# Experts' output rows: one scatter for each piece, or summed in SBUF and scattered block by block

## The chip, the core and the metric

The kernel runs on one core of a Trainium2 chip, in one launch. The metric is device time in microseconds (us); smaller is better. PE is the matrix engine (TensorE), PEld its loading of the stationary operand, DVE VectorE, ACT ScalarE, POOL GpSimd, SP SyncE, which here only issues DMAs.

## What is computed

Two transformer layers on 1024 rows (32 x 32) of 256 float32 values. Each layer is an attention block and a feed-forward block:

```python
x = x + _L0_attn_ref(_L0_cond_ref(x, ...), ...)
x = x + _L0_ffn_ref(_L0_cond2_ref(x, ...), ...)
x = x + _L1_attn_ref(_L1_cond_ref(x, ...), ...)
x = x + _L1_ffn_ref(_L1_cond2_ref(x, ...), ...)
```

The change touches the last one, `_L1_ffn_ref`: a mixture of 16 experts with hidden width 128, of which each row uses two, and a shared expert that every row uses.

```python
probs = softmax(xt @ Wr.T + bias)                # 1024 x 16
topk_val, topk_idx = top_k(probs, 2)
w = topk_val / (sum(topk_val) + 1e-9)
g = einsum('th,ehi->tei', xt, Wg)                # hidden width i = 128
u = einsum('th,ehi->tei', xt, Wu)
y = einsum('tei,eih->teh', silu(g) * u, Wd)
routed = einsum('tke,tk,teh->th', one_hot(topk_idx), w, y)
shared = (silu(xt @ sWg) * (xt @ sWu)) @ sWd
return routed + shared
```

## The kernel before

**Blocks and pieces.** Only the two experts of a row are computed. The 1024 rows with two experts each make 2048 gated rows, sorted by expert and cut into NB = 16 blocks of P = 128. An expert's rows may begin and end inside a block, so one block may need several experts. A *piece* is one block with one expert. Going through blocks and experts in order, as in a merge, there are always NP = 16 + 16 - 1 = 31 pieces. Piece j is of expert `ex[j]` and of block `j - bx[j]`; both numbers come from the data, are computed on the chip into `eb` and loaded into registers of PE and DVE. A piece runs all 128 rows of its block through its expert, and only the rows that belong to this expert are used afterwards.

**Before the loop.** The attention rows that the experts work on go out to `od` in DRAM (`rows_out`, tile `o`). `tok_` has the row number of each sorted row, `slot_` tells whether the expert was the row's first or second choice. `pick(b)` lets POOL gather the 128 rows of block b from `od` into `xg[b]` (L1469): nine gathers in front of the loop, the other seven in the loop, each behind one piece's products. All experts' weights stand in SBUF as `ew` (6 MB).

**The loop over pieces** (one turn of `for j in range(NP)` each):

- For j < 16, PE turns block j of `xg` (`xt`, L1565) and DVE copies it to `xT` (L1567). These 16 turns are called the first half here, the other 15 the second.
- DVE copies the piece's block out of `xT` to `xs` (L1576), with an address from a register.
- PE multiplies it by gate and up weights into `gu` (L1579, two instructions in the code, four in the trace), the weights' address from a register.
- ACT takes the Silu (`hb`, L1591), DVE multiplies by the up half (`hb`, L1592). These are the gated rows.
- PE turns them (`ht`, L1594), ACT copies the result (`hT`, L1596).
- PE multiplies by the down weights into `y` (L1598); its PSUM pool `yp` has two buffers.
- DVE (odd pieces, L1601) or ACT (even pieces, L1603) copies `y` to `yb`, one of 12 buffers.
- POOL scatters `yb` to the rows of `ys_d` in DRAM (L1608), one row for each token and choice. The row numbers are column k of `to`; rows that belong to another piece of the block have a number beyond the table and are dropped by the bounds check.

`places()` computes `to` from the sorted order on DVE (L1519 to L1544), at piece 2.

**The shared expert** is done in two halves of 512 rows. `shared_in(n)` makes gate and up products, Silu and product (L1325 to L1341), `shared_out(n)` the four down products and their addition to `acc`, which already holds the rest of the sum (L1347, L1351). Half 0 is begun ahead of the loop, with the product of its hidden rows on POOL (L1338), and added at piece 2. Half 1 comes with the loop's end.

**The end.** `weigh()` makes the two weights of each row. Eight DMAs load `ys_d` back, 128 tokens with both choices each (L1628, in turn on the SP and the ACT queue). Sixteen DVE instructions multiply by the weights and add to `acc` (L1632), and eight DMAs write the output (L1635).

**The order of instructions** on each engine comes from a scheduler that sees all of the program. The code adds orders where it wants others: `behind(first, *later)` says that each of `later` stands behind `first` in its engine's queue, with no wait of its own, and `products` writes a sum of products in one bank. `declare_no_dep` says that two instructions with overlapping memory are not to wait for each other. Pools hand their buffers out in turn, so an instruction also waits for the last reader of its buffer.

Of the kernel before, what the change touches and what calls it, by code (L numbers as in the profile page):

```python
# [128 lines left out]
def tile_layers(ctx: ExitStack, tc: tile.TileContext, i: dict, out: bass.AP):  # L129
# [60 lines left out]
    def products(groups, ends=None):  # L190


        last = None
        for ps, pairs in groups:
            for j, (a, b) in enumerate(pairs):
                mm_ = te.matmul(ps, lhsT=a, rhs=b, start=j == 0, stop=j == len(pairs) - 1)  # L196
                if j == 0 and last is not None:
                    tc.add_manual_dep(mm_.ins, last.ins.name, in_order, reason="one open sum per bank")
            last = mm_
            if ends is not None:  # L200
                ends.append(mm_)
        return last
# [843 lines left out]
    with tc.tile_pool(name="w1", bufs=1, reuse_waits="tile") as wp:  # L1046
# [269 lines left out]
        with (  # L1316
# [3 lines left out]
            def small(name, shape, dt=F32):  # L1320
                return hp.tile(list(shape), dt, name=name)

            hs = small("h", (P, CH)), small("up", (P, CH))

            def shared_in(n, pool, tag, eng):  # L1325
                ns = slice(n * CH, (n + 1) * CH)
                pair = []
                for f in (NE, NE + P):
                    ps = pool.tile([P, CH], F32, tag=tag, name=tag)
                    products([(ps, [(wfo[:, k, f : f + P], AVT[:, k, ns]) for k in range(2)])])  # L1330
                    pair.append(ps)
# [20 lines left out]

            w12 = small("w12", (P, 2, NG))
            eb = small("eb", (1, NP), I32)
            to = small("to", (P, NP), I32)
            xT = hp.tile([P, NB, D], F32, name="xT")
            with (
                tc.tile_pool(name="mm5", bufs=3, space=bass.MemoryType.PSUM, reuse_waits="tile") as mm,
# [6 lines left out]
                def rows_out(g):  # L1365

                    po = mm.tile([P, CH], F32, tag="mm", name="mm")
                    products([(po[:, :D], [(AVT[:, k, g * P : (g + 1) * P], wo2[:, k, :]) for k in range(2)])])
                    o = sp.tile([P, D], F32, tag="o", name="o")
                    s.copy(o, po[:, :D])  # L1370
                    (nc.sync, s)[g % 2].dma_start(od[g * P : (g + 1) * P, :], o)

# [140 lines left out]
            with (  # L1513
# [3 lines left out]
                tc.tile_pool(name="y5", bufs=2, space=bass.MemoryType.PSUM, reuse_waits="tile") as yp,  # L1517
            ):
                def places():  # L1519

                    of = small("of", (P, NB, NE))
                    of_ = v.tensor_tensor(
                        of,
                        starts.unsqueeze(1).broadcast_to([P, NB, NE]),
                        C("row").unsqueeze(2).broadcast_to([P, NB, NE]),
                        ALU.is_le,
                    )
                    behind(loaded[1][-1], of_)
                    pn = small("pn", (P, NB))
                    v.tensor_reduce(pn, of, AX.X, ALU.add)  # L1530
                    v.tensor_tensor(pn, pn, C("block1"), ALU.add)
                    v.scalar_tensor_tensor(slot_, slot_, float(NT), tok_, ALU.mult, ALU.add)
                    v.tensor_scalar(slot_, slot_, -SKIP, None, ALU.add)
                    mine = small("mine", (P, NP, NB))
                    v.tensor_tensor(
                        mine,
                        pn.unsqueeze(1).broadcast_to([P, NP, NB]),
                        C("piece").rearrange("p (j b) -> p j b", b=NB),
                        ALU.is_equal,
                    )  # L1540
                    v.tensor_tensor(mine, mine, slot_.unsqueeze(1).broadcast_to([P, NP, NB]), ALU.mult)
                    tof = small("tof", (P, NP))
                    v.tensor_reduce(tof, mine, AX.X, ALU.add)
                    v.tensor_scalar(to, tof, SKIP, None, ALU.add)  # L1544

                def weigh():

# [6 lines left out]
                    v.reciprocal(su, su)  # L1554
                    v.tensor_tensor(w12, w12, su.unsqueeze(1).broadcast_to([P, 2, NG]), ALU.mult)

                put, ybs, gus = [], [], []
                for j in range(NP):
                    if j == 2:
                        places()  # L1560
                        shared_out(0, first_h, yp, "y")
                    if j < NB:
                        pt = xp.tile([P, CH], F32, tag="xt", name="xt")
                        for k in range(2):
                            turned = te.transpose(pt[:, k * P : (k + 1) * P], xg[j][:, k * P : (k + 1) * P], ident)  # L1565
                            behind(gus[j - 2] if j > 1 else loaded[0][-1], turned)
                        v.tensor_copy(xT[:, j, :], pt[:, :D])  # L1567
                    w = ew[:, bass.ds(ex[j], 1), :].rearrange("p a n -> p (a n)")
                    at_b = nc.s_assert_within(
                        j - bx[j],  # L1570
                        max(0, j - NE + 1),
                        min(j, NB - 1),
                        skip_runtime_bounds_check_because="a piece's number is its block's and its expert's together",
                    )
                    x = sp.tile([P, 1, D], F32, tag="xs", name="xs")
                    v.tensor_copy(x, xT[:, bass.ds(at_b, 1), :])  # L1576
                    pg = gp.tile([P, CH], F32, tag="gu", name="gu")
                    for k in range(2):
                        mm_ = te.matmul(  # L1579
                            pg[:, :D],  # L1580
                            lhsT=x[:, 0, k * P : (k + 1) * P],
                            rhs=w[:, k * D : (k + 1) * D],
                            start=k == 0,
                            stop=k == 1,
                        )
                    gus.append(mm_)
                    if len(xg) < NB:
                        pick(len(xg))
                        tc.add_manual_dep(picked[-1].ins, mm_.ins.name, waits, reason="no long row of gathers")
                    h = sp.tile([P, P], F32, tag="hb", name="hb")  # L1590
                    s.activation(h, pg[:, :P], AF.Silu)  # L1591
                    v.tensor_tensor(h, h, pg[:, P:D], ALU.mult)  # L1592
                    ph = tp.tile([P, CH], F32, tag="ht", name="ht")
                    te.transpose(ph[:, :P], h, ident)  # L1594
                    hT = sp.tile([P, P], F32, tag="hT", name="hT")
                    s.copy(hT, ph[:, :P])  # L1596
                    py = yp.tile([P, CH], F32, tag="y", name="y")
                    te.matmul(py[:, :D], lhsT=hT, rhs=w[:, 2 * D :], start=True, stop=True)  # L1598
                    yb = sp.tile([P, D], F32, tag="yb", name="yb", bufs=12)
                    if j % 2:  # L1600
                        v.tensor_copy(yb, py[:, :D])  # L1601
                    else:
                        s.copy(yb, py[:, :D])  # L1603
                    ybs.append(yb)
                    if j >= 2:
                        for k in range(len(put), j + 1):
                            put.append(
                                g_.indirect_dma_start(  # L1608
                                    out=ys_d,
                                    out_offset=bass.IndirectOffsetOnAxis(ap=to[:, k : k + 1], axis=0),  # L1610
                                    in_=ybs[k],
                                    in_offset=None,
                                    bounds_check=2 * NT - 1,
                                    oob_is_err=False,
                                )
                            )
                weigh()
                shared_out(1, shared_in(1, gp, "gu", v), yp, "y")
                behind(picked[-1], *put)
                for j, a in enumerate(put):  # L1620
                    for b in put[:j]:
                        tc.declare_no_dep(a.ins, b.ins, reason="a row is written by one piece")
                ys = ys_d.rearrange("(k g p) d -> g p k d", k=2, p=P)
                y2s = []
                for g in range(NG):
# [83 lines left out]
```

## Time and profile before

| what | us | from |
|---|---|---|
| median of three runs | 644.38 | 643.24, 644.38, 644.47 |
| the profiled execution, its own time | 649.91 | the run |
| span of its trace | 647.7 | the page |
| stages ahead of the last attention's end | 538 | busy time in stretches |
| routing, order of rows, first gathers | 538 to 573 | the same |
| pieces 4 to 15 | 573 to 602 | the same |
| pieces 16 to 30 | 602 to 628.5 | the same |
| last pieces' scatter, loads, weighted sums, output | 628.5 to 647.7 | the same |

Each row of the profile's groups names a line, an engine, an operation, the tiles (out<-in) with their shapes, the number of instructions, their busy time and mean length, and what ended the engine's idle time ahead of them. The rows of the last 100 us that the change touches:

```profile
L1608 POOL DMA_INDIRECT ys_d<-yb,to x31 | 30.8, 995 | 22.3 <-ACT hT L1596 7.4 <-DVE yb L1601 5.5 <-ACT yb L1603 5.0
L1576 DVE COPY xs<-xT 128x256 f32 (+1 forms) x31 | 10.3, 355 | 10.1 <-PE gu L1579 9.8 <-DVE hb L1592 0.3
L1601 DVE COPY yb<-y 128x256 f32<-128x256 f32 x15 | 6.4, 424 | 7.6 <-PE gu L1579 3.5 <-PE y L1598 3.5
L1603 ACT COPY yb<-y 128x256 f32<-128x256 f32 x16 | 6.0, 372 | 11.0 <-PE y L1598 6.6 <-remote 3.3 <-issue 1.2
L1351 DVE TENSOR_TENSOR acc<-acc,y 128x256 f32<-128x256 f32 x8 | 3.4, 421 | 1.8 <-PE y L1347 1.7
```

In a timeline a row is a time from the span's start, a length, the engine, the line, the operation and the tiles, and in brackets how long the engine was idle ahead of it and what ended that. The clock (PEclk) is the share of full speed that PE was granted.

### The profile page before, as it was taken

The page shows a single profiled execution, that of the slowest core. Times are in us where ns is not written, and L with a number is a line of the kernel's source. Part 1 is how long each engine was busy: PE and PEld are TensorE (multiplying, and loading weights), DVE is VectorE, ACT ScalarE, POOL GpSimd, SP SyncE. Part 2 cuts the span into 40 slices and gives each one's busy share as a digit, 9 for nine tenths or more (in the row PEclk, how much of TensorE's full clock was granted, in tenths as well). Part 3 has the DMA queues.
Part 4 walks back from the last instruction along what each step waited for, and adds up shares of the span by engine and source line. Part 5 has one row for each costly group of instructions (what it writes and reads, how often), then busy time and mean ns, then how long its engine had stood idle before and what let it go on. Part 6 is the DMA issues. An engine that isn't in the chain of part 4 may idle for free.

```text
span 647.7 us, 9218 instructions
## 1 busy us (share of the span) xinstructions
PE 579.4 (89%) x3302; PEld 449.0 (69%) x3302; DVE 377.9 (58%) x880; ACT 185.0 (29%) x503; POOL 195.7 (30%) x279
## 2 busy tenths in 40 slices
PE   3989999999999998999999999996788889686992
PEld 1667778688778886788878886785565666464660
DVE  4656675865956939433292139554566685642535
ACT  1312232332312213122031103233456454121440
POOL 5014001523530049950000000007465300655550
PEclk9979999999999999999999999997799989797997
DMA  6962300555441000000000046014221101221115
GB/s 176 361 214 27 64 2 26 153 128 134 116 131 39 0 14 1 1 2 17 0 1 1 1 161 293 1 54 119 57 66 58 49 2 66 74 61 46 33 50 194
DMA packets 29884, 48.47 MB, mean 75 GB/s; under 512 B 8249, under 2 KB 21966, under 8 KB 29008
## 3 DMA queue, kind: packets, MB, share of 16 engines
q1 hardware_dynamic: 19405, 30.23, 13.7%
q0 software_dynamic: 5904, 15.39, 9.2%
q10 hardware_dynamic: 4531, 2.28, 1.2%
q8 instruction: 26, 0.43, 0.3%
q14 instruction: 18, 0.15, 0.1%
HBM read 36.84 MB, written 13.01 MB: 77 GB/s over the span
## 4 chain that ended last, share of the span: by engine, by line
PE 70%; DVE 16%; issue 4%; ACT 3%; DMA 3%; POOL 2%; another core or an unknown queue 1%; ACTq 0%; SPq 0%; DVEq 0%; POOLq 0%
PE ff L196 30%; PE mm L196 11%; PE gu L1579 4%; PE y L1598 3%; PE sc L1157 3%; PE tr L477 3%; DVE vblk L427 2%; PE sc L444 2%; PE po L1191 2%; PE mm L939 2%; DVE kb L437 2%; ACT sm L1172 2%; DVE AVT L1225 1%; PE tr L470 1%; POOL xg L1469 1%
## 5 line engine op out<-in xcount | busy, mean ns | idle before, releaser
L1098 POOL DMA_INDIRECT kv<-rows_d,at x40 | 39.2, 979 | 173.8 <-DVE rsm L1012 152.3
L662 POOL COPY rr<-raw 88x256 f32<-88x256 f32 x64 | 29.4, 493 | 95.8 <-PE tr L525 48.8
L594 DVE SCALAR_TENSOR_TENSOR th<-th,ff 128x512 f32<-128x512 f32 x32 | 21.8, 683 | 38.1 <-ACT th L593 38.1
L437 DVE TENSOR_TENSOR kb<-KT,con 128x1024 f32<-128x1024 f32 x28 | 34.0, 1234 | 12.3 <-ACT KT L539 6.0
L1608 POOL DMA_INDIRECT ys_d<-yb,to x31 | 30.8, 995 | 22.3 <-ACT hT L1596 7.4
L1579 PE MATMUL gu<-ew,xs 128*128 x124 | 36.4, 415 | 0.7 <-DVE xs L1576 0.7
L593 ACT ACTIVATE th<-ff 128x512 f32<-128x512 f32 x32 | 19.1, 597 | 59.5 <-PE ff L196 56.1
L196 PE MATMUL ff<-x,w_g 128*128 128x256 f32 x128 | 35.6, 391 | 0.0
L196 PE MATMUL ff<-x,w_u 128*128 128x256 f32 x128 | 34.9, 386 | 0.0
L196 PE MATMUL ff<-y,f_w_gate 128*128 128x256 f32 x128 | 31.5, 381 | 0.0
L196 PE MATMUL ff<-y,f_w_up 128*128 128x256 f32 x128 | 31.1, 381 | 0.3 <-DVE th L594 0.3
L1172 ACT ACTIVATE sm<-sm,mx 128x160 f32<-128x160 f32 x64 | 26.8, 420 | 11.7 <-DVE mx L1170 8.6
L196 PE MATMUL ff<-h,d_Wd 128*128 128x256 f32 x128 | 29.8, 381 | 0.0
L1598 PE MATMUL y<-ew,hT 128*128 x62 | 21.9, 436 | 7.7 <-issue 4.2
L196 PE MATMUL ff<-h,f_w_down 128*128 128x256 f32 x128 | 28.3, 379 | 0.0
L1157 PE MATMUL sc<-KT,qz 128*128 128x160 f32 x128 | 25.9, 335 | 2.6 <-issue 2.4
L1579 PEld LDWEIGHTS gu<-ew,xs 128*128 128x128 f32 x124 | 24.3, 209 | 5.6 <-DVE xs L1576 1.1
L1191 PE MATMUL po<-PT,kv 128*128 128x256 f32 x64 | 19.8, 432 | 9.4 <-ACT PT L1188 7.5
L1166 DVE SCALAR_TENSOR_TENSOR sm<-bad,sc 128x320 f32<-128x320 bf16 x32 | 15.5, 485 | 21.5 <-PE sc L1157 8.0
L196 PEld LDWEIGHTS ff<-x,w_g 128*128 128x128 f32 x128 | 22.8, 189 | 7.4 <-issue 4.9
L595 DVE SCALAR_TENSOR_TENSOR h<-th,ff 128x512 f32<-128x512 f32 x32 | 21.8, 680 | 9.4 <-PE ff L196 9.1
L196 PEld LDWEIGHTS ff<-x,w_u 128*128 128x128 f32 x128 | 23.5, 190 | 5.4 <-issue 2.2
(421 smaller groups left out, 1314.5 us busy)
## 6 DMA issues: line engine op xcount, KB each, us to landing
ew<-in_L_ffn_W SPq DMA_DIRECT2D x1, 6144.0 KB
rows_d<-rr SPq DMA_DIRECT2D x32, 176.0 KB
x<-in_x SPq DMA_DIRECT2D x4, 256.0 KB
w_u<-in_L_cond_Wu SPq DMA_DIRECT2D x1, 1024.0 KB
w_g<-in_L_cond_Wg SPq DMA_DIRECT2D x1, 1024.0 KB
d_Wd<-in_L_cond_Wd SPq DMA_DIRECT2D x1, 1024.0 KB
f_w_gate<-in_L_ffn_w_gate SPq DMA_DIRECT2D x1, 1024.0 KB
f_w_up<-in_L_ffn_w_up SPq DMA_DIRECT2D x1, 1024.0 KB
```

The costliest lines, as they stand in the source:

```text
L196: mm_ = te.matmul(ps, lhsT=a, rhs=b, start=j == 0, stop=j == len(pairs) - 1)
L437: v.tensor_tensor(kb, KT[:, m, js].rearrange("p (b k) -> p b k", b=4).unsqueeze(2).broadcast_to([P, 4, 8, 32]), m8.unsqueeze(1).unsqueeze( ...
L594: v.scalar_tensor_tensor(flat(t), flat(t), 1.0, flat(pg), ALU.add, ALU.mult)
L595: v.scalar_tensor_tensor(flat(h[:, f : f + 2]), flat(t), 0.5, flat(pu), ALU.mult, ALU.mult)
L662: g_.tensor_copy(r[:, :, j].rearrange("p o g d -> p g o d"), raw[j].rearrange("p (g a o d) -> a p g o d", g=4, a=8, d=32)[a],)
L1098: got = g_.indirect_dma_start(out=kv[:, a, :], out_offset=None, in_=rows_d, in_offset=bass.IndirectOffsetOnAxis(ap=at[:, g, a : a + 1], ax ...
L1157: mm_ = te.matmul(ps[:, h, :], lhsT=q.qz[:, b, h].rearrange("p g t -> p (g t)"), rhs=q.KT[:, b, :], start=True, stop=True,)
L1172: exp_ = s.activation(sm[:, h], sm[:, h], AF.Exp, bias=mx[:, h : h + 1], accum_out=q.su[:, b, h : h + 1])
L1191: mm_ = te.matmul(q.po[:, b, : 2 * P], lhsT=q.kv[:, b, P:], rhs=PT[:, j, :], start=True, stop=False)
L1579: mm_ = te.matmul(pg[:, :D], lhsT=x[:, 0, k * P : (k + 1) * P], rhs=w[:, k * D : (k + 1) * D], start=k == 0, stop=k == 1,)
L1598: te.matmul(py[:, :D], lhsT=hT, rhs=w[:, 2 * D :], start=True, stop=True)
L1608: g_.indirect_dma_start(out=ys_d, out_offset=bass.IndirectOffsetOnAxis(ap=to[:, k : k + 1], axis=0), in_=ybs[k], in_offset=None, bounds_ch ...
```

## The change

- The pieces of one block are summed in SBUF. A new tile `yall` holds 16 blocks of 128 rows x 256 and is zeroed by four POOL memsets. For each piece a DVE instruction adds `y`, multiplied by the piece's column of `own`, to the piece's block of `yall`, whose address comes from a register. `own` has a 1 for the rows of the block that are the piece's and a 0 for the others. This instruction takes the place of the copy to `yb` on DVE or ACT.
- A block is scattered when its last piece can have been added: block b behind piece b + 15. There are 16 scatters for 31, all in the second half, with no rows left out. `to` has one column for a block. `places()` computes `own` as a maximum, loses three DVE instructions, and stands behind piece 1.
- For odd pieces j of the first half, the product `y` of piece j - 1 (`yd` at that place in the code) is ordered behind the turn `ht` of piece j's gated rows, so PE has both turns of a pair ahead of both products.
- `shared_in` takes an instruction that its products are to stand behind; for half 1 it is the last piece's `y`.
- The tile `o` takes its buffers from those of `xs`.

```diff
-            def shared_in(n, pool, tag, eng):
+            def shared_in(n, pool, tag, eng, after=None):
...
-                    products([(ps, [(wfo[:, k, f : f + P], AVT[:, k, ns]) for k in range(2)])])
+                    for k in range(2):
+                        up_ = te.matmul(ps, lhsT=wfo[:, k, f : f + P], rhs=AVT[:, k, ns], start=k == 0, stop=k == 1)
+                        if after:
+                            behind(after, up_)
...
-            to = small("to", (P, NP), I32)
+            to, own = small("to", (P, NB), I32), small("own", (P, NP))
+            yall = hp.tile([P, NB, D], F32, name="yall")
+            for b in range(0, NB, 4):
+                g_.memset(yall[:, b : b + 4, :], 0.0)
...
-                    o = sp.tile([P, D], F32, tag="o", name="o")
+                    o = sp.tile([P, 1, D], F32, tag="xs", name="o")[:, 0, :]
...
-                    v.scalar_tensor_tensor(slot_, slot_, float(NT), tok_, ALU.mult, ALU.add)
-                    v.tensor_scalar(slot_, slot_, -SKIP, None, ALU.add)
...
-                    v.tensor_tensor(mine, mine, slot_.unsqueeze(1).broadcast_to([P, NP, NB]), ALU.mult)
-                    tof = small("tof", (P, NP))
-                    v.tensor_reduce(tof, mine, AX.X, ALU.add)
-                    v.tensor_scalar(to, tof, SKIP, None, ALU.add)
+                    v.tensor_reduce(own, mine, AX.X, ALU.max)
+                    v.scalar_tensor_tensor(to, slot_, float(NT), tok_, ALU.mult, ALU.add)
...
                     if j == 2:
-                        places()
                         shared_out(0, first_h, yp, "y")
...
-                    te.transpose(ph[:, :P], h, ident)
+                    ht_ = te.transpose(ph[:, :P], h, ident)
+                    if j % 2 and j < NB:
+                        behind(ht_, yd)
...
-                    te.matmul(py[:, :D], lhsT=hT, rhs=w[:, 2 * D :], start=True, stop=True)
-                    yb = sp.tile([P, D], F32, tag="yb", name="yb", bufs=12)
-                    if j % 2:
-                        v.tensor_copy(yb, py[:, :D])
-                    else:
-                        s.copy(yb, py[:, :D])
...
+                    yd = te.matmul(py[:, :D], lhsT=hT, rhs=w[:, 2 * D :], start=True, stop=True)
+                    ys_.append((j, at_b, py))
+                    if j == 1:
+                        places()
+                    while j >= 1 and ys_:
+                        k, at_k, py = ys_.pop(0)
+                        to_k = yall[:, bass.ds(at_k, 1), :].rearrange("p a n -> p (a n)")
+                        kept_.append(
+                            v.scalar_tensor_tensor(to_k, py[:, :D], own[:, k : k + 1], to_k, ALU.mult, ALU.add)
+                        )
+                    if j >= NE - 1:
+                        b = j - NE + 1
+                        put.append(
+                            g_.indirect_dma_start(
+                                out=ys_d,
+                                out_offset=bass.IndirectOffsetOnAxis(ap=to[:, b : b + 1], axis=0),
+                                in_=yall[:, b, :],
+                                in_offset=None,
+                            )
+                        )
                 weigh()
-                shared_out(1, shared_in(1, gp, "gu", v), yp, "y")
+                shared_out(1, shared_in(1, gp, "gu", v, yd), yp, "y")
...
+                    for x in kept_[j + NE :]:
+                        tc.declare_no_dep(x.ins, a.ins, reason="a later block's rows")
```

More of the change, by code (lines that the diff above doesn't have):

```diff
@@ L1555, in weigh @@
                     v.tensor_tensor(w12, w12, su.unsqueeze(1).broadcast_to([P, 2, NG]), ALU.mult)
-                put, ybs, gus = [], [], []
+                put, kept_, ys_, gus = [], [], [], []
                 for j in range(NP):
                     if j == 2:
-                        places()
                         shared_out(0, first_h, yp, "y")
@@ L1597, in tile_layers @@
                     py = yp.tile([P, CH], F32, tag="y", name="y")
-                    te.matmul(py[:, :D], lhsT=hT, rhs=w[:, 2 * D :], start=True, stop=True)
-                    yb = sp.tile([P, D], F32, tag="yb", name="yb", bufs=12)
-                    if j % 2:
-                        v.tensor_copy(yb, py[:, :D])
-                    else:
[L1603 to L1615, printed above, removed]
+                    yd = te.matmul(py[:, :D], lhsT=hT, rhs=w[:, 2 * D :], start=True, stop=True)
[16 more added lines that the diff above has]
+                                in_offset=None,
                             )
+                        )
                 weigh()
-                shared_out(1, shared_in(1, gp, "gu", v), yp, "y")
+                shared_out(1, shared_in(1, gp, "gu", v, yd), yp, "y")
                 behind(picked[-1], *put)
@@ L1621, in tile_layers @@
                     for b in put[:j]:
-                        tc.declare_no_dep(a.ins, b.ins, reason="a row is written by one piece")
+                        tc.declare_no_dep(a.ins, b.ins, reason="a row is in one block")
+                    for x in kept_[j + NE :]:
+                        tc.declare_no_dep(x.ins, a.ins, reason="a later block's rows")
                 ys = ys_d.rearrange("(k g p) d -> g p k d", k=2, p=P)
```

## The prediction

> **What bounds the kernel now.** I read the page's chain of waits first, then busy time in stretches, then the timeline of the expert loop and of the end.
>
> ```profile
> PE 70%; DVE 16%; issue 4%; ACT 3%; DMA 3%; POOL 2%; another core or an unknown queue 1%; ACTq 0%; SPq 0%; DVEq 0%; POOLq 0%
> ...
> 572.90:602.00 29.10, 22.13 (x95) 15.98 (x95) 11.54 (x38) 6.64 (x25) 15.80 (x16) 0.88 0.14 46
> 602.00:628.50 26.50, 26.50 (x115) 18.12 (x114) 11.96 (x38) 11.79 (x41) 15.81 (x16) 1.00 0.13 45
> ```
>
> The chain is PE's for 70%. The stretches (columns: PE, PEld, DVE, ACT, POOL, PE clock, DMA share, GB/s) split the loop: pieces 16 to 30 (602 to 628.5) keep PE busy throughout, pieces 4 to 15 (572.9 to 602) leave it idle for 7.0 us. So only the first half and the end can give anything. One step of two pieces there:
>
> ```profile
> 577.28 1.89 PE L1579 MATMUL gu<-ew,xs 128*128 x8
> 579.21 0.28 ACT L1591 ACTIVATE hb<-gu 128x128 f32<-128x128 f32 x1 [0.59 <-PE gu L1579]
> 579.52 0.29 DVE L1592 TENSOR_TENSOR hb<-hb,gu 128x128 f32<-128x128 f32 x1 [0.57 <-ACT hb L1591]
> 579.74 0.70 PE L1598 MATMUL y<-ew,hT 128*128 x2
> 580.27 0.27 PE L1594 MATMUL ht<-ident,hb 128*128 128x128 f32 x1
> 580.39 0.59 DVE L1576 COPY xs<-xT 128x256 f32 x2
> 580.47 0.37 ACT L1603 COPY yb<-y 128x256 f32<-128x256 f32 x1 [0.79 <-PE y L1598]
> 580.74 0.27 ACT L1596 COPY hT<-ht 128x128 f32<-128x128 f32 x1
> 581.06 0.70 PE L1598 MATMUL y<-ew,hT 128*128 x2 [0.52 <-ACT yb L1603]
> 581.60 1.89 PE L1579 MATMUL gu<-ew,xs 128*128 x8
> ```
>
> A step takes 581.60 - 577.28 = 4.32 us. The second piece's hidden rows are turned (580.27) only after the first piece's product `y`, and their copy `hT` stands on ACT behind `yb`; PE waits 0.52 us for that. The inputs `xs` of the next pair are ready long before they are wanted.
>
> ```profile
> 588.34 1.22 PE L1598 MATMUL y<-ew,hT 128*128 x2 [3.48 <-issue]
> 589.36 3.62 PE L1579 MATMUL gu<-ew,xs 128*128 x8
> ```
>
> Two steps are longer: 581.60 to 589.36 and from there to 596.99 are 7.76 and 7.63 us, 6.75 more than 2 x 4.32. PE stands 3.48 us with no waiter named, then runs at half clock. I take this hole for an event of the profiled execution: that one took 649.91 us (span 647.7 and 2.2 around it), the median is 644.38, 5.53 less. What I sum up below lies outside the hole, so I take it from the median: against the profile's own 649.91 it would be the same difference.
>
> ```profile
> 627.88 0.70 PE L1598 MATMUL y<-ew,hT 128*128 x2
> 628.25 0.29 DVE L1592 TENSOR_TENSOR hb<-hb,gu 128x128 f32<-128x128 f32 x1 [1.36 <-ACT hb L1591]
> 628.42 1.02 PE L196 MATMUL gu<-AVT,wfo 128*128 128x512 f32 x2
> 630.25 0.59 PE L1598 MATMUL y<-ew,hT 128*128 x2
> 631.64 0.98 POOL L1608 DMA_INDIRECT ys_d<-yb,to  x1 [1.34 <-ACT yb L1603]
> 633.83 1.98 ACTq L1628 DMA_DIRECT2D y<-ys_d  x4
> 637.46 3.25 DVE L1632 SCALAR_TENSOR_TENSOR acc<-y,w,acc 128x256 f32<-128x256 f32 x8 [1.25 <-DMA y<-ys_d]
> 641.52 3.25 DVE L1632 SCALAR_TENSOR_TENSOR acc<-y,w,acc 128x256 f32<-128x256 f32 x8 [0.81 <-DMA y<-ys_d]
> ```
>
> The end is one chain: last product, copy, last scatter (631.64), eight loads of `ys` (from 633.83), and DVE waiting for the second four of them until 641.52.
>
> **The change part by part.** *The memsets* (L1362, four of 128x1024 on POOL). Rows: a POOL memset of 128x128 takes 0.205 us, one of 128x1 0.10, so 0.8 ns an element, 0.94 us each; by POOL's copy L662 (256 elements, 0.493 us) 2.0 us each. Together 3.8 to 7.9 us. They wait for the last attention product, which ends at 538.2, and so end by 542 to 546.1; POOL's next work is the first gather at 553.42. That idle time hides them, with 7 us to spare; without it they would cost their full length. Nothing.
>
> *`places`* loses L1533, L1541 and L1544 (0.17 + 0.66 + 0.17 us of DVE, by their rows). The DVE row behind them, `hb` at 561.26, starts where ACT has just finished (560.95 + 0.28), and the first `shared_out` product waits at 565.77 for POOL's `h`, which stands behind nine gathers in any case. Nothing.
>
> *Scatters*: 31 become 16, 15 x 0.995 us less on POOL. Nobody waits for any but the last. Nothing, except there.
>
> *ACT and DVE*: sixteen ACT copies (0.37) and fifteen DVE copies (0.42) go; DVE gets 31 sums L1612. No row shows one with an address from a register. Nearest: L1351, also 128x256 with one operand in PSUM, 0.42; L1632, the same operation, 0.48. That is 13.0 to 14.9 us for 6.4, in 55.6 us of which DVE is busy 23.5: no bound in sum, but in the first half the built order puts each sum in front of an `xs` copy, a new wait.
>
> *First-half step, with the pair's own lines.* `hb` of the second piece ends at 579.81; its turn follows 0.07 later (as 578.94 to 579.01 a piece earlier), 579.88, now ahead of `y`. `y` starts 0.11 later (the pitch of the transposes), 579.99, and takes 0.59 to 0.70 (both stand above): 580.58 to 580.69. The sum starts 0.03 later and takes 0.42 to 0.48: 581.03 to 581.20. `xs` takes 0.28 (median of L1576), less 0.08 where DVE instructions overlap (two L1567 copies of 0.42 take 0.76): 581.23 to 581.48. `gu` follows after 0.07, and loses 0.10 because its weights can't be loaded ahead (0.70 against 0.59 again): 581.40 to 581.65 where it was 581.60. Per step that is between 0.20 less and 0.05 more. The bounds lie further out: if the sums hid wholly, PE alone would set the step (turn 579.88, `hT` 580.19 to 580.46, second `y` 580.51, next `gu` 0.53 later, 581.04), 0.56 less; if nothing hid, see the slower rival. I take 0.12, between the chain's two ends but nearer the short one, since the `y` weights are ready ahead there. Pieces 4 to 14 make five steps: -0.6 us (-2.8 to +2.2). Pieces 2 and 3 keep `xs` in front of the sums, and in the second half `xs` runs three pieces ahead: nothing there.
>
> *The end.* `gu` of `shared_in(1)` no longer stands in front of the last turn. `hb` ends at 628.54, turn 628.61, `hT` 0.36 later for 0.27 (as on the rows before: 627.20, 627.56), `y` 629.29 instead of 630.25, done 629.99; sum to 630.44-630.50; POOL 0.28 later (629.04 to 629.32 on the scatter before): 630.75 instead of 631.64, 0.89 earlier. The last scatter now carries a whole block: the DMA view shows a full 128-row transfer busy for 0.4 to 0.7 us, one of few rows for 0.2; I charge 0.25 (0 to 0.5). All loads and the two L1632 rows come 0.64 earlier. The four `gu` products moved behind (3.4 us) put the last `acc` rows at 636.9 instead of 636.2, between the new first load (636.8) and the rest; the first eight L1632 then end at 640.9, when the second loads land. Hidden, with no cover left: at most 0.1 lost. -0.64 us (-0.9 to -0.3).
>
> Sum: 644.38 - 0.6 - 0.64 = 643.1 us.
>
> POOL and DVE do exclude each other: the longest `xs` copy took 1.98 us, from inside the time of POOL's `h` (564.44 to 565.71). The Trainium skill says so too ("SBUF — State Buffer", section "Who interferes with whom"): an fp32 SBUF copy on VectorE and a GpSimd instruction lock each other out, and the first to issue keeps the ports; an operation with one SBUF input, as the new sums are, does not contend. By that rule `xs` of piece 2, now behind the first sum, comes up at about 564.4 together with `h` and may push it by 0.3 us, and with it the product that waits for it: 643.4. The trace shows the lock, not this order of issue.
>
> **The rivals.** *Slower: the sums hold up `xs`.* In each first-half step PE waits for `y`, sum, `xs`, one behind the other. Costs not in my chain: an `xs` copy under a POOL DMA instruction took 0.51 (the pair from 576.07, 0.70 for two), 0.23 more; three register addresses at 0.036 + 0.075 us (DVE queue rows of L1576) add 0.33 if they aren't hidden. Step 4.20 + 0.56 = 4.76, five times 0.44 more than before: +2.2, less the end's 0.64: 645.9. It decides from a step of 4.45 on, where five steps eat the end's gain. For it: the order of the DVE queue; against: DVE has free time in each step and the registers are set while the engine runs.
>
> *PE sets the step.* 5 x 0.56 + 0.64 = 3.4 less: 640.9. For it: ACT's wait is gone; against: the chain above.
>
> *The hole belongs to every run, and falls with the early scatters that POOL issues through it.* 6.75 less as well: 636.4. Against: the median is already 5.53 below the profiled execution.
>
> *It does nothing*: steps as long as before, half the end eaten: 644.1.
>
> **How the numbers follow.** Forecast 48%, slower rival 28%, PE-set step 14%, nothing 6%, hole 4%. A measurement of this kernel can tell about 0.2% (1.3 us) from no change. The forecast's own range is 642.2 to 644.2, and its 643.1 stands on that edge: 28 of its 48 count as faster, 20 as same. Faster: 28 + 14 + 4 = 46%; same: 20 + 6 + 3 of the slower rival = 29%; slower 25%. The range runs from the PE-set step to the slower rival, 640.9 to 645.9.
>
> **What would show it.** Right: steps of two pieces of about 4.2 us, PE's `gu` in them released by `xs`, `xs` by the sum; second half at 1.65 us a piece (621.28 to 622.93 before); last scatter about 0.9 us after the last `y`'s end and one tail load earlier by 0.6. Wrong: steps over 4.4 or under 4.0; gathers later than memsets allow; another hole, which only a timed run can set aside.

## The result, and the profile after

The changed kernel took 637.94 us (median of four runs, 637.57 to 640.51), the kernel before 644.42 (four runs, 643.24 to 649.03). The ratio is 0.9882, 95% interval 0.9842 to 0.9923: 6.5 us faster, where 1.3 were forecast. The profiled execution took 637.68, its span is 635.9.

The busy time in stretches of the changed kernel, cut at the gate products `gu` of piece 4, those of piece 14 and the end of the last ones (columns: length, then PE, PEld, DVE, ACT and POOL busy, PE clock, DMA share, GB/s):

```profile
567.81:589.53 21.72, 19.92 (x92) 13.23 (x90) 13.34 (x41) 5.11 (x20) 2.83 (x3) 1.00 0.07 22
589.53:616.36 26.83, 26.76 (x115) 18.27 (x115) 16.65 (x48) 8.47 (x32) 12.68 (x13) 1.00 0.17 60
616.36:635.90 19.54, 7.40 (x21) 3.50 (x21) 10.05 (x24) 1.14 (x3) 2.91 (x3) 0.82 0.56 188
```

Pieces 4 to 14 take 21.72 us. Before they took 28.42 (572.88 to 601.31). The rest of the loop takes 26.83 (26.6 before) and what lies behind the last gate products 19.54 (19.82 before). So of the 11.8 us between the two spans 6.7 are in this one stretch, and it has no hole: PE's clock is 1.00 throughout. Of the rest, 0.8 are in pieces 0 to 3 and 4.3 lie ahead of the loop, the latter in stages that the change doesn't touch: the first gate products start at 554.58 instead of 558.84.

One step of two pieces, from the timeline of the changed kernel:

```profile
576.44 1.97 PE L1580 MATMUL gu<-ew,xs 128*128 x8 [0.23 <-DVE xs L1577]
...
578.75 0.29 DVE L1593 TENSOR_TENSOR hb<-hb,gu 128x128 f32<-128x128 f32 x1 [0.57 <-ACT hb L1592]
...
579.10 0.33 PE L1595 MATMUL ht<-ident,hb 128*128 128x128 f32 x1
...
579.26 1.27 PE L1602 MATMUL y<-ew,hT 128*128 x4
...
579.99 0.48 DVE L1612 SCALAR_TENSOR_TENSOR yall<-y,own,yall 128x256 f32 x1 [0.28 <-PE y L1602]
580.39 0.28 DVE L1577 COPY xs<-xT 128x256 f32 x1
580.67 0.48 DVE L1612 SCALAR_TENSOR_TENSOR yall<-y,own,yall 128x256 f32 x1
...
580.82 1.97 PE L1580 MATMUL gu<-ew,xs 128*128 x8 [0.28 <-DVE xs L1577]
```

The wait of 0.52 us for `hT` is gone, as the change says, and a wait of 0.28 for the input copy `xs` stands there: the copy comes behind the sum (579.99), and the sum behind the first `y`. A step takes 580.82 - 576.44 = 4.38 us; the five steps are 4.31, 4.32, 4.38, 4.32 and 4.38. They were 4.32 to 4.40 before, where there was no hole. **The steps are no shorter.**

The end, from the timeline:

```profile
617.79 0.70 PE L1602 MATMUL y<-ew,hT 128*128 x2 [0.41 <-issue]
...
619.29 0.97 POOL L1617 DMA_INDIRECT ys_d<-yall,to  x1 [0.39 <-DVE yall L1612]
...
621.73 1.99 ACTq L1637 DMA_DIRECT2D y<-ys_d  x4
...
625.25 0.48 DVE L1641 SCALAR_TENSOR_TENSOR acc<-y,w,acc 128x256 f32<-128x256 f32 x1 [0.89 <-DMA y<-ys_d]
...
626.32 2.46 DVE L1641 SCALAR_TENSOR_TENSOR acc<-y,w,acc 128x256 f32<-128x256 f32 x6
629.19 3.78 DVE L1641 SCALAR_TENSOR_TENSOR acc<-y,w,acc 128x256 f32<-128x256 f32 x9 [0.41 <-DMA y<-ys_d]
```

From the end of the last gate products to that of the last `y` it takes 2.13 us instead of 2.94, from the last scatter to the first load 2.44 instead of 2.18. Seven weighted sums come before the second loads and nine behind them; before it was eight and eight.

### The profile page after: what moved, and what is told of

Its sections match the earlier page's. It is cut to its first block, busy times and chain, and to the rows that moved or that the text cites. A ratio compares the mean times of both kernels' runs of the same rounds, so it can differ in the third digit from the quotient of the medians.

```text
span 635.9 us, 9278 instructions
## 1 busy us (share of the span) xinstructions
PE 576.7 (91%) x3302; PEld 445.7 (70%) x3302; DVE 383.4 (60%) x893; ACT 179.3 (28%) x487; POOL 184.0 (29%) x268
## 4 chain that ended last, share of the span: by engine, by line
PE 68%; DVE 18%; issue 4%; ACT 4%; DMA 3%; POOL 2%; another core or an unknown queue 1%; SPq 0%; DVEq 0%; ACTq 0%; POOLq 0%
PE ff L196 31%; PE mm L196 10%; PE gu L1580 4%; PE tr L477 3%; PE y L1602 2%; PE sc L1157 2%; DVE kb L437 2%; PE po L1191 2%; DVE vblk L427 2%; PE mm L939 2%; ACT sm L1172 2%; PE sc L444 1%; PE tr L470 1%; POOL xg L1476 1%
## 5 line engine op out<-in xcount | busy, mean ns | idle before, releaser
L1580 PE MATMUL gu<-ew,xs 128*128 x124 | 34.8, 401 | 2.1 <-DVE xs L1577 1.3
L1580 PEld LDWEIGHTS gu<-ew,xs 128*128 128x128 f32 x124 | 22.9, 199 | 7.6 <-PE y L1602 3.2
L196 PEld LDWEIGHTS ff<-y,f_w_up 128*128 128x128 f32 x128 | 24.0, 190 | 4.0 <-DVE th L594 0.7
L196 PEld LDWEIGHTS ff<-y,f_w_gate 128*128 128x128 f32 x128 | 24.0, 190 | 4.0 <-issue 0.8
```

What stands on the lines that cost most here:

```text
L1580: mm_ = te.matmul(pg[:, :D], lhsT=x[:, 0, k * P : (k + 1) * P], rhs=w[:, k * D : (k + 1) * D], start=k == 0, stop=k == 1,)
```

## The experiments

Each job ran on one chip together with the kernel before, and the jobs fell on five chips, which the table numbers. The *stretch* is from piece 4's gate products to piece 14's, in the profiled execution. The first runs' chip isn't known. E1 in the text is e1_before_again, and so on. No chip ran in two jobs, so what is called a difference of chips below could also be one of jobs. The ratio is the recorded comparison with the runs of the kernel before in the same job; it is not the quotient of the two medians, and on chip 4 it gives a gain up to 2.5 us smaller than they do.

| chip | run | stretch, us | median, us | ratio to before, same chip (95%) |
|---|---|---|---|---|
| first runs | before | 28.42 | 644.42 | |
| | after | 21.72 | 637.94 | 0.9882 (0.9842 to 0.9923) |
| 1 | before, e1_before_again | 29.50 | 644.74 | |
| | e2_no_early_scatters | 21.65 | 638.60 | 0.9904 (0.9870 to 0.9938) |
| | e3_turns_only | 27.96 | 643.49 | 0.9973 (0.9938 to 1.0009) |
| | e4_early_scatters_back | 34.37 | 650.32 | 1.0107 (1.0056 to 1.0158) |
| 2 | before | | 628.98 | |
| | e5_fewer_rows | 21.73 | 629.43 | 0.9990 (0.9964 to 1.0016) |
| | e6_paced | 21.70 | 630.13 | 1.0005 (0.9974 to 1.0035) |
| | e7_no_turn_order | 21.17 | 629.60 | 0.9999 (0.9974 to 1.0025) |
| | e8_inputs_first | 19.28 | 625.69 | 0.9940 (0.9910 to 0.9971) |
| 3 | before, e9_before_here | 21.65 | 629.92 | |
| | e10_early_again | 21.73 | 627.47 | 0.9976 (0.9950 to 1.0002) |
| | e11_fewer_rows_again | 21.72 | 629.40 | 0.9999 (0.9974 to 1.0025) |
| | e12_paced_again | 21.70 | 629.28 | 1.0001 (0.9975 to 1.0028) |
| 4 | before | | 650.38 | |
| | after, e13_after_here | 21.70 | 638.66 | 0.9859 (0.9805 to 0.9914) |
| | e14_inputs_first_again | 19.27 | 638.41 | 0.9836 (0.9792 to 0.9880) |
| | e15_paced_third | 21.71 | 640.22 | 0.9882 (0.9833 to 0.9932) |
| | e16_fewer_rows_third | 35.89 | 653.50 | 1.0072 (1.0037 to 1.0106) |
| 5 | before | | 628.92 | |
| | after, e17_after_twin | 21.71 | 629.69 | 1.0005 (0.9976 to 1.0034) |
| | e18_inputs_first_third | 19.27 | 625.95 | 0.9935 (0.9912 to 0.9959) |

### Is the hole in every run?

> The kernel before, unchanged, profiled once more. Theory A (the stall of PE in the middle of the first half is in every run of the kernel before): the stretch from the gate products of piece 4 to those of piece 14 takes about 28.4 us again (601.31 - 572.88), two of its five steps being 7 us or longer, and the run takes about 644 us. Theory B (the stall belonged to that one profiled execution, and the gain comes from the new order of the products and the end): the stretch takes 5 x 4.35 = 21.8 us, and the run still takes 644 us, so that the 6 us are to be looked for elsewhere.

E1, no edit. The hole is there again, at the same place (this profiled execution took 647.81 us): the steps are 4.40, 4.32, 6.94, 8.09 and 5.75, the stretch 29.50. Its timeline:

```profile
582.84 0.37 ACT L1603 COPY yb<-y 128x256 f32<-128x256 f32 x1 [1.77 <-PE ht L1594]
...
584.27 0.27 ACT L1596 COPY hT<-ht 128x128 f32<-128x128 f32 x1 [1.06 <-remote]
584.59 1.22 PE L1598 MATMUL y<-ew,hT 128*128 x2 [2.67 <-issue]
584.78 0.98 POOL L1608 DMA_INDIRECT ys_d<-yb,to  x1 [0.30 <-issue]
...
585.60 3.62 PE L1579 MATMUL gu<-ew,xs 128*128 x8
```

ACT waits for results of PE whose instruction ended long before ("remote": the profile finds no local instruction that released it), PE then waits for ACT, and POOL issues one scatter after the other with 0.30 us between. The gate products behind it take 3.62 us instead of 1.89. Theory A.

### Do the early scatters make it?

> The kernel before without the scatters of pieces 0 to 13 (their rows of the output are wrong; the table is filled with other rows beforehand, long ahead of the loop). Theory A1 (the stall comes from the row of scatters that POOL issues back to back in the first half): it is gone, the stretch from piece 4 to piece 14 takes 21.8 us and the time falls by about 6.6 to 638. Theory A2 (the stall is there whatever POOL does, for example from instructions being fetched at that point): stretch 28.4 us, time 644. Theory B: stretch 21.8, time 644.

```diff
+        for k in range(2):
+            nc.sync.dma_start(ys_d[k * NT : (k + 1) * NT, :], i["x"])
...
-                    if j >= 2:
-                        for k in range(len(put), j + 1):
+                    if j >= 14:
+                        for k in (j,):
```

E2: the stretch is 21.65 and the time 6.1 us less than before: A1.

> The changed kernel with fourteen more scatters of one block each, into a table that nobody reads, at the places where the kernel before has its first fourteen (half of the rows are beyond the bound, as there). Theory A1: the stall comes back, a PE wait of some us with no waiter named between 575 and 595, and the time rises by about 6.6 to 644. Theory A2 or B: the stretch from piece 4 to 14 stays at 21.8 us and the time at 638.

```diff
+                    if 2 <= j < 14:
+                        for k in range(len(early), j + 1):
+                            early.append(
+                                g_.indirect_dma_start(
+                                    out=zz_d,
+                                    out_offset=bass.IndirectOffsetOnAxis(ap=to[:, k : k + 1], axis=0),
+                                    in_=xg[k],
+                                    in_offset=None,
+                                    bounds_check=NT - 1,
...
+                behind(picked[-1], *early)
+                behind(early[-1], *put)
```

E4: the hole is back, and longer than in the kernel before: the stretch is 34.37, one of its steps 13.90. From the timeline:

```profile
579.50 0.27 ACT L1601 COPY hT<-ht 128x128 f32<-128x128 f32 x1 [2.62 <-remote]
...
581.28 0.98 POOL L1618 DMA_INDIRECT zz_d<-xg,to  x1 [0.30 <-issue]
...
586.55 0.28 ACT L1593 ACTIVATE hb<-gu 128x128 f32<-128x128 f32 x1 [6.79 <-remote]
...
587.20 0.48 PE L1596 MATMUL ht<-ident,hb 128*128 128x128 f32 x1 [3.01 <-issue]
```

ACT waits 2.62 and then 6.79 us for PE's results while the scatters go on. With E2 this settles that on this chip early scatters make the hole, in either kernel. The time, 650.32, is 6 us above the 644 that was expected: this hole is larger than that of the kernel before.

### What the order of the turns is worth

> The kernel before with nothing but the two turns of a pair ahead of its two products. Theory A1: the scatters are as before, so the stall stays; the steps lose the 0.52 us that PE waits for the second copy, at most 0.3 to 0.5 us each over five steps, and the time is 642 to 643. Theory B (the order makes the gain): 638 to 639.

```diff
-                    te.transpose(ph[:, :P], h, ident)
+                    ht_ = te.transpose(ph[:, :P], h, ident)
+                    if j % 2 and j < NB:
+                        behind(ht_, yd)
```

E3: where there is no hole the steps are 3.85 and 3.86 us, 0.46 less than before; the hole stays (7.39 and 8.54). The ratio, 0.9973, can't be told from no change, so the order alone did not make the gain.

> The changed kernel without the order of the turns. Theory S (the sums in front of the input copies set the step, so that the order brings nothing): 638 within 0.7, steps of 4.3 to 4.4 us. Theory O (the order brings in the changed kernel what it brought alone, 4.32 - 3.86 = 0.46 us a step): steps of 4.8 us, 640 to 641.

```diff
-                    if j % 2 and j < NB:
-                        behind(ht_, yd)
```

E7: neither theory's steps; they are 4.21 to 4.28. In the changed kernel the order makes the five steps together 0.54 us longer (21.71 for 21.17), and the one from piece 2 to piece 4 shorter (5.58 in E17, 6.38 here). The ratio, 0.9999, is that of the changed kernel on such a chip, 1.0005.

### What holds the steps: the sums ahead of the input copies

> The changed kernel with the input copies of pieces 4 to 15 ahead of the sums of the pair before them in DVE's queue, nothing else. Theory S: the step falls from 4.35 to the 3.86 us that the order of the turns gave alone, six steps by 0.49, so 635.0. Theory P (products and their own latencies set the step and DVE is in time anyway): 638, steps of 4.35.

```diff
-                    v.tensor_copy(x, xT[:, bass.ds(at_b, 1), :])
+                    xs_ = v.tensor_copy(x, xT[:, bass.ds(at_b, 1), :])
+                    if j % 2 and 3 < j < NB:
+                        behind(xs_, *kept_[j - 3 : j - 1])
```

E8: the steps are 3.85 and 3.86, as theory S has it. That chip's times were all some 16 us lower than those of the first two jobs, the kernel before included, so nothing could be said of the sum until the two kernels ran side by side.

> The changed kernel with the input copies ahead of the sums, beside the changed kernel on one chip: six steps by 0.49 us, 2.9 us less than the changed kernel, on either kind of chip.

E14: steps of 3.85 again, but 638.41 beside 638.66 us: six runs each, which spread from 635.2 to 643.8. This alone leaves it open.

> The changed kernel with the input copies ahead of the sums. Theory S (DVE's order sets the changed kernel's steps): 3.86 us a step for 4.35, 2.5 us less than the changed kernel in the same job, and less than the kernel before on a chip without the stall too. Theory W (what is saved in the loop is lost again behind it): the same time as the changed kernel, though the steps are shorter.

E18: 625.95 us, where the changed kernel took 629.69 (twelve runs, 625.90 to 633.09) and the kernel before 628.92. The ratio to before is 0.9935 (0.9912 to 0.9959), and this interval does not touch the changed kernel's on the same chip. Of the 3.7 us between the two medians the profiles place 2.4 in the stretch (19.27 for 21.71); where the rest lies they don't show. Its step:

```profile
567.07 1.89 PE L1582 MATMUL gu<-ew,xs 128*128 x8
567.09 1.07 DVE L1614 SCALAR_TENSOR_TENSOR yall<-y,own,yall 128x256 f32 x2 [0.29 <-issue]
...
569.82 1.27 PE L1604 MATMUL y<-ew,hT 128*128 x4
...
570.18 0.48 DVE L1577 COPY xs<-xT 128x256 f32 x2
...
570.92 0.59 PE L1582 MATMUL gu<-ew,xs 128*128 x2
```

Both copies are done at 570.66, the sums lie beside the gate products (567.09), and PE goes from `y` (569.82 + 1.27 = 571.09 by the modelled end) straight into the next `gu`. This is the fastest version: ahead of both kernels on chip 5 and ahead of the kernel before on all three chips where it ran.

### Back to back, or the rows that are moved?

> The changed kernel with the fourteen extra scatters, of which the bound now lets through only the rows below 256 of 2048, an eighth instead of a half. Theory R (the rows that the DMA engines write make the stall): it shrinks with the rows, a quarter of the 12.4 us that the extra scatters cost, 641. Theory I (POOL's issuing of one scatter behind the other makes it, whatever is moved): 649 to 651 as with half of the rows.

```diff
-                                    bounds_check=NT - 1,
+                                    bounds_check=NT // 4 - 1,
```

> The changed kernel with eight extra scatters, those of pieces 6 to 13, each waiting for its own piece's last product, so that there are two in a step of 4.35 us and POOL has no row of them to issue back to back. Theory I1 (a row of scatters issued back to back makes the stall): no wait without a name, steps of 4.3 to 4.4 us, 638. Theory I2 (every scatter in the first half costs its part): 8/14 of 12.4 us, 645.

```diff
-                    if 2 <= j < 14:
-                        for k in range(len(early), j + 1):
+                    if 6 <= j < 14:
+                        for k in (j,):
...
+                        tc.add_manual_dep(early[-1].ins, yd.ins.name, waits, reason="one scatter a piece")
```

E5 and E6: no hole in either, but both ran on a chip where the kernel before took 628.98 us, so they told nothing. The next job asked whether such a chip has the hole at all.

> The kernel before once more, profiled on the chip that the next three run on too. Two jobs gave 644.7 and 629.0 us for it. Theory C (the stall of the first half is there on some chips only): where it takes about 629 us, the stretch from piece 4 to 14 takes 5 x 4.32 = 21.6 us and PE has no wait without a name in it; where it takes about 644, the stretch takes 28 us. Theory D (the stall is everywhere, and a chip is faster or slower in the other stages): 28 us in both.

E9: it hasn't. The stretch of the kernel before there, in one line of the stretches and two of POOL's timeline:

```profile
556.06:577.71 21.65, 19.05 (x92) 13.97 (x92) 11.14 (x37) 6.46 (x25) 14.20 (x15) 1.00 0.18 60
```

```profile
574.66 0.99 POOL L1608 DMA_INDIRECT ys_d<-yb,to  x1 [0.30 <-issue]
575.95 0.99 POOL L1608 DMA_INDIRECT ys_d<-yb,to  x1 [0.30 <-ACT hT L1596]
```

The same scatters, 1.29 us from one to the next, and the stretch takes 21.65 us at a full clock: theory C.

> The changed kernel with fourteen extra scatters of half a block each, as in the run that took 650.3. Where the kernel before stalls: about 5 us more than the kernel before. Where it doesn't, by theory C: no stall here either, within 1 us of the kernel before; by theory D: 5 us more everywhere.

> The same with an eighth of the rows, on the chip of the run with half of them. Theory R (rows written): a quarter of the stall of the run with half of the rows. Theory I (POOL issues scatters back to back): the same stall. On a chip without a stall: the time of the kernel before, within 1 us, which tells nothing of the two.

> The changed kernel with eight extra scatters, two to a step. On a chip with a stall, theory I1 (only a row of scatters back to back makes it): no stall, 6 to 7 us less than the kernel before. Theory I2 (each early scatter its part): over half of the stall of the run with fourteen. On a chip without one: the time of the kernel before, within 1 us.

E10 to E12: none of the three has a hole on this chip (21.70 to 21.73), not even the fourteen scatters of E4. They take what the kernel before takes, and tell the theories apart no further.

> The changed kernel itself, beside the kernel before on one chip once more. Theory C (the gain is the stall under the row of early scatters, which only some chips have): where the kernel before takes about 644, 6 to 7 us less; where it takes about 629, within 1.5 us of it. A chip that stalls shows itself by the kernel before, at about 644.

E13: by its time this chip has the hole: the kernel before takes 650.38 us, the changed one 638.66. That is 11.7 less by the medians and about 9 by the ratio, more than the 6 to 7 expected. The kernel before was not profiled here; E16 below shows a hole on this chip.

> The changed kernel with eight extra scatters, two to a step, each waiting for its own piece. Where the kernel before stalls: theory I1 (only a row of POOL DMAs back to back stalls) gives the changed kernel's time within 1 us; theory I2 (each early scatter costs its part) 6 to 7 us more than the changed kernel. Elsewhere: the changed kernel's time, which tells nothing.

> The changed kernel with fourteen extra scatters back to back that move an eighth of their rows. Where the kernel before stalls: theory R (the rows written make the stall) gives 3 us more than the changed kernel; theory I (the issuing back to back) 12 us more, as the run with half of the rows. Elsewhere: the changed kernel's time, which tells nothing.

E15 and E16: on this chip the fourteen scatters with an eighth of their rows take 653.50, 14.8 us more than the changed kernel, and the stretch 35.89. The eight paced ones take 640.22, which is 1.6 more where at most 1 was expected, but the interval overlaps the changed kernel's and the stretch is the same. From the timelines, first the one with few rows, then POOL's in the paced one:

```profile
581.46 0.27 ACT L1601 COPY hT<-ht 128x128 f32<-128x128 f32 x1 [3.34 <-remote]
...
589.58 0.98 POOL L1618 DMA_INDIRECT zz_d<-xg,to  x1 [0.30 <-issue]
590.02 0.28 ACT L1593 ACTIVATE hb<-gu 128x128 f32<-128x128 f32 x1 [8.30 <-remote]
```

```profile
577.44 1.03 POOL L1618 DMA_INDIRECT zz_d<-xg,to  x1 [1.42 <-PE y L1603]
578.78 1.00 POOL L1618 DMA_INDIRECT zz_d<-xg,to  x1 [0.30 <-issue]
581.76 0.98 POOL L1618 DMA_INDIRECT zz_d<-xg,to  x1 [1.98 <-PE y L1603]
583.05 0.99 POOL L1618 DMA_INDIRECT zz_d<-xg,to  x1 [0.31 <-issue]
```

So **it takes the row of scatters, and few rows are enough**: with an eighth of the rows ACT waits 8.30 us, and pairs of scatters with a pause of about 2 us between them cost nothing that shows (stretch 21.71). That the paced ones are eight and not fourteen doesn't explain it: in E4 and E16 ACT's first late wait (to 579.50 and to 581.46) ends before the seventh scatter of the row starts. Half of the rows was never run on this chip; E4's 12.4 us for it, beside the changed kernel of the first runs, comes from another, so whether more rows make the hole longer is not shown. POOL takes 0.98 us for a scatter of few rows and of many. The Trainium skill explains this in "Perfetto Trace Analysis", section "DMA Instruction — SWDGE (GPSIMD)": the end that the profile shows is when POOL has written its descriptors, not when the rows are moved. The two runs agree with that.

> The changed kernel once more, to compare with the next run on one chip. Where the kernel before takes about 629 us (no stall): within 1.5 us of it, by the steps of 4.35 us for 4.33, a second half 0.2 us longer and an end 0.3 us shorter. Where it takes 644 or more: 6 to 12 us less than it.

E17: 629.69 beside 628.92: on a chip without the hole the changed kernel **gains nothing** (1.0005, 0.9976 to 1.0034).

## Why the prediction was wrong

- **The hole: the step that failed.** "I take this hole for an event of the profiled execution", because that execution lay 5.53 us above the median and the hole was 6.75. The runs showed the hole in both profiles of the kernel before on such chips (28.42 and 29.50 us for the stretch), and its price in the timed runs: 6.1 us (E2), with 6.5 for the whole change (the result) and 9 to 12 on chip 4. The 5.53 needs no hole to explain it: twenty runs of the kernel before on chip 1 took 640.38 to 650.37 us. Part of such a spread lies ahead of the loop, whose first `gu` stands at 558.84 in one profile of the kernel before and at 555.98 in the other; where the rest lies isn't shown. Two numbers of one size were taken for one thing.
- **The rival that named it** (the hole is in every run and falls with the early scatters, 636.4 us) was 1.5 us from the result and had 4%. Its mechanism was right; the only objection to it was the 5.53. Its number had 1.2 us in it for the steps and the end, which did not come: the hole alone, 644.4 - 6.7, gives 637.7. The trace had a second sign, a wait for "remote" of 7.58 us under fourteen gathers that POOL issued back to back:

```profile
453.73 0.95 POOL L1098 DMA_INDIRECT kv<-rows_d,at  x1 [0.31 <-issue]
457.20 0.49 DVE L1166 SCALAR_TENSOR_TENSOR sm<-bad,sc 128x320 f32<-128x320 bf16 x1 [7.58 <-remote]
```

  The changed kernel still has that one, on a chip with holes (E13, first below) and not on one without (E17):

```profile
446.34 0.95 POOL L1098 DMA_INDIRECT kv<-rows_d,at  x1 [0.30 <-issue]
447.47 0.49 DVE L1166 SCALAR_TENSOR_TENSOR sm<-bad,sc 128x320 f32<-128x320 bf16 x1 [3.91 <-remote]
447.59 0.95 POOL L1098 DMA_INDIRECT kv<-rows_d,at  x1 [0.30 <-issue]
...
450.30 0.37 ACT L1121 COPY KT<-tr 128x256 f32<-128x256 f32 x1 [5.72 <-remote]
```

```profile
443.22 0.95 POOL L1098 DMA_INDIRECT kv<-rows_d,at  x1 [0.30 <-issue]
443.92 0.49 DVE L1166 SCALAR_TENSOR_TENSOR sm<-bad,sc 128x320 f32<-128x320 bf16 x1 [1.33 <-PE sc L1157]
444.47 0.95 POOL L1098 DMA_INDIRECT kv<-rows_d,at  x1 [0.30 <-issue]
```

  From the first of these gathers to the first product of L1221 it takes 27.8 to 30.2 us in all ten profiles of the first runs and of chips 1 and 4, and 23.6 to 24.6 in all ten of chips 2, 3 and 5, whatever the kernel. This hole goes with the chips as the other does; no run took the gathers away, so that they make it is not shown.
- **The steps** (0.12 us less each, five times): the new wait was named rightly, the size wrongly. The five steps take 21.71 us in e17 and 21.65 in e9, nothing for -0.6. The chain came out at its long end: `y` starts 0.16 us behind the turn for 0.11, the sum takes 0.48 for 0.42 to 0.48, PE waits 0.28. The choice "nearer the short end" had no row behind it that bore on `y`'s length: its weights were ready, and the sum still started 0.73 behind `y`'s start.
- **PE sets the step** was priced at 0.56 and is 0.46 to 0.49 once the copies go first (E8). The slower rival's mechanism, sums that hold up `xs`, is there; its price, 0.44 a step, isn't: the addresses in registers cost nothing that shows.
- **The end** (-0.64): the last `y` comes 0.81 earlier (0.96 forecast) and the last scatter's larger transfer takes 0.26 longer (0.25). But from the first load on it takes 14.2 to 14.8 us in three profiles of the changed kernel, 13.7 to 14.3 in three of the one before. From the end of the last gate products to the end of the program it takes 19.54, 19.67 and 20.20 for 19.82, 19.62 and 20.19, about -0.1. The four `gu` moved behind push the `acc` rows back, and "at most 0.1 lost" was too little: a ninth sum waits behind the second loads.
- **What held:** the memsets take 0.951 us each (0.94 estimated) and end at 537.9, 11 us ahead of the first gather; the sums take 0.48 us with their register addresses; `places` cost nothing that shows. POOL's `h` locks a DVE copy out but not the sum, as the rule of the Trainium skill says ("SBUF — State Buffer", section "Who interferes with whom"):

```profile
560.36 1.27 POOL L1341 TENSOR_TENSOR h<-h,up 128x512 f32<-128x512 f32 x1
...
560.60 0.48 DVE L1612 SCALAR_TENSOR_TENSOR yall<-y,own,yall 128x256 f32<-128x256 f32 x1 [0.71 <-DMA xg<-od,tok]
561.00 0.80 DVE L1577 COPY xs<-xT 128x256 f32 x1
```

  Under POOL's `h` the sum, with one operand in SBUF, takes its usual 0.48, the copy 0.80 for 0.28. But `h` was first and the copy waited, not the other way round as the forecast had it.
- **The two terms together**, -1.2 us in the forecast, can be seen by themselves on a chip without the hole: in E17's job the medians of the two kernels differ by +0.8 us, and the ratio's interval goes from -1.5 to +2.1. The time alone doesn't refute -1.2; the steps and the end in the traces do.

## What to carry to other kernels

A wait that the profile can't explain ("remote", or an engine that stands at "issue") deserves a second look at what all other engines do at that moment, and a search of the same trace for another of its kind, before it is put down to one execution. A row of indirect DMAs that POOL issues back to back beside a chain of short PE, ACT and DVE steps cost 6 to 15 us on some chips here and nothing on others. Fewer of them, or a pause behind every second one, avoided it, and a gain found on one chip should be measured on another. When two orders are changed at once, look first at what DVE does: the turns alone would shorten a step by 0.46 us, the sums in front of the copies take it back, and one line of order gives both.

## What the runs showed that was not expected

- Chips fall in two kinds for this kernel: 628.9 to 629.9 us on three of them, 644.7 and 650.4 on two, and 644.4 in the first runs. The hole of the first half and the one under the fourteen gathers are on the slower kind alone. They are not all of the difference: between E13 and E17, the same kernel without the first hole, the spans differ by 9.1 us, 6.6 of them in the stage of these gathers and 4.6 between it and the first expert gather, with 2.1 the other way elsewhere.
- On chip 4 fourteen scatters back to back cost the changed kernel 14.8 us (E16 beside E13), more than the 9 to 12 that the kernel before takes there above the changed one.
- Not shown: what is late in it. ACT and DVE get PE's results some us after the records end PE's instructions, and those ends are modelled; whether PE stood still or its signals came late, and what sets the two kinds of chips apart, no run here tells. Late instructions stay possible too: the stretch has transfers of 16 and of 8 KB in the DMA queues named "instruction", which take 1.0 to 1.5 and 0.3 to 0.5 us with the hole and 1.0 to 1.4 and 0.3 to 0.6 without it, but when they were asked for the traces don't tell.
